# Expert attention of a two-layer vision tower: projection biases moved into the evacuation of the values, gate logits by column strips

## The chip, the cores and the metric

The kernel runs on one core of one Trainium2 chip, in one launch. The metric is the device time of one execution in microseconds. TensorE is called PE here, VectorE DVE, ScalarE ACT, GpSimd POOL and SyncE SP, as in the profile; PEld is TensorE's weight load, which overlaps its matmuls.

## The reference

A tokenizer turns 128 images into 64 tokens of 256 features each. Layer 0 is an attention with ReLU scores and then a feed-forward part that is itself an attention with experts; layer 1 is a linear attention and a mixture of experts. Everything is float32. The change lies in the feed-forward part of layer 0, which the program calls `expert_attention`. The reference writes it so (B = 128 images, T = 64 tokens, D = 256 features, E = 4 experts, C = 4 chunks of DC = 64 features, H = 2 heads of 32):

```python
xn = layernorm(x) * norm_w
gate = softmax(xn @ router_w.T + router_b, axis=-1)            # per token, over 4 experts
xc = xn.reshape(B, T, C, DC)
qkv = einsum('btcd,ekd->btcek', xc, qkv_w)                      # q, k, v per chunk, expert, head
attn = softmax(einsum('bcehtd,bcehsd->bcehts', q, k) * scale, axis=-1)
y = einsum('bcehts,bcehsd->bcehtd', attn, v)
y = einsum('btced,eod->btceo', y, proj_w) + proj_b              # proj_b: one bias of 64 per expert
out = einsum('btceo,bte->btco', y, gate).reshape(B, T, D)
return residual + out @ out_w.T
```

## The kernel before

The stages run one after another: tokenizer, ReLU attention, expert attention, linear attention, routing, experts. The residual stream `h2` stays in SBUF through the first three.

In `expert_attention` the unit of work is a **pair** of images: 2 x 64 tokens fill the 128 partitions. There are 64 pairs, and four pairs make a **block**, for which layer norm and gate are computed ahead. The projection `proj_w` is folded into the value weights before the loop (`wvp`, lines 766 to 783), so that a pair's values `v` are already projected. A softmax weight is multiplied by the gate of its expert (`weights`, lines 956 to 961), so that one sum over four experts and two heads (`mixed`) gives the gated output `z`; `output` multiplies it by `out_w` and adds it to `h2`. Softmax weights of a row sum to one, and so the bias `proj_b` reaches the output as gate times bias times `out_w`. The kernel before adds it there: before the loop it makes `bn` (bias times `out_w`, 4 x 256, placed at four row offsets), per block it transposes the gates into `gT` (lines 875 to 880), and per pair one more matmul (line 998) adds `gT` times `bn` to the output's PSUM tile `po`.

The order of the loop is written out by hand under a manual schedule, and each engine works through its own list in that order. One turn of the loop for pair p (`cur`), with the next pair (`new`) and the one before (`old`):

1. PE transposes `old`'s weights of head 0 (`pt`, line 970), ACT copies them out (973).
2. PE computes the scores `sc` (934); DVE takes maximum and difference of each head (946, 947).
3. PE computes queries and keys of `new` (`pqk`, 902), transposes `old`'s weights of head 1, computes the other half of `pqk`; ACT copies them out (906) and takes the exponents of the two heads (950).
4. DVE sums the exponents of each head and takes the reciprocal (953, 954); POOL scales (960, 961). Steps of other blocks that carry the place names "DVE", "DVE2" stand on DVE between or behind the two heads' sums: `statistics` (812, 813), `logits_less_max` (861 to 863), `sums` of the gate (869, 870).
5. PE mixes (`pz`, 983; ACT copies `z`, 991), computes `new`'s values into four PSUM tiles `pv` (914), and then `old`'s output `po` (997, 998). The values of chunk half `fc` = 0 (the first two `pv`) are copied to SBUF by ACT, those of `fc` = 1 by DVE (both on line 923). DVE adds `po` to `h2` (999).
6. PE does steps of other blocks at the place "PE" (transposes `ptx` 843, logits `pg` 854, gate transpose `pgt` 877).

All PSUM tiles but the scores come from one pool of four buffers of one bank each (tag "pq"), taken in turn, so that a matmul into a tile waits until the tile that is four places ahead of it has been read out. `po` takes the buffer of the first `pv`. A `pv` tile is 128 x 512 float32: its partitions are (expert pair, token), its free axis is (image, expert of the pair, head, 64 features).

The gate's logits of a block (line 854) are eight matmuls that hold `xT` (128 x 128) as weights and move four router columns each.

At which turn a block's steps stand is set by the `at` calls (lines 1014 to 1031) with n = 4b, the block's first pair; keys below zero are run before the loop ("first").

Of the kernel before, what the change touches and what calls it, by code (L numbers as in the profile page):

```python
# [11 lines left out]
F32 = mybir.dt.float32  # L12
# [7 lines left out]
P = 128  # L20
B = 128
T = 64
D = 256
# [30 lines left out]
def bcast(ap, axis, n):  # L54

    v = ap.unsqueeze(axis)
    shape = list(v.shape)
    shape[axis] = n
    return v.to_broadcast(shape)
# [670 lines left out]
def expert_attention(c, hd, normw, wr, br, wqkv, wvT, wproj, bproj, wout):  # L730
# [3 lines left out]
    tc, nc, h2 = c.tc, c.nc, c.h2  # L734
    SCALE = float(1.0 / np.sqrt(np.float32(32)))
    NP = B // 2
    NB = 4
    with (
# [7 lines left out]
    ):  # L746
        nw = wp.tile([P, 2], F32, name="nw")
        nc.sync.dma_start(nw, normw)
        wrs = wp.tile([P, 2, 4], F32, name="wrs")
        nc.sync.dma_start(wrs, wr.rearrange("(c p) e -> p c e", p=P))  # L750
        brs = wp.tile([P, 4], F32, name="brs")
        nc.sync.dma_start(brs, br.partition_broadcast(P))
        w = wp.tile([P, 2 * D], F32, name="w")
        bp2 = wp.tile([P, 4], F32, name="bp2")
        for k in range(2):
            nc.sync.dma_start(w[k * 64 : k * 64 + 64, :], wqkv)
            nc.sync.dma_start(bp2[k * 64 : k * 64 + 64, :], bproj)
        wv = wp.tile([32, 8, 64], F32, name="wv")
        nc.scalar.dma_start(wv, wvT)
        wpj = wp.tile([32, 8, 64], F32, name="wpj")  # L760
# [1 line left out]
        wo = wp.tile([P, 2, D], F32, name="wo")  # L762
# [7 lines left out]
        pv = psq.tile([P, 2, D], F32, tag="pq", name="pwv")  # L770
        for k in range(2):
            for e in range(4):
                for h in range(2):
                    r = (e % 2 * 2 + h) * 64
# [4 lines left out]
                        start=True,  # L779
                        stop=True,  # L780
                    )
        wvp = wp.tile([P, 2, D], F32, name="wvp")
        nc.vector.tensor_copy(wvp, pv)


        pb = psq.tile([4, D], F32, tag="pq", name="pb")
        for fc in range(2):
            nc.tensor.matmul(pb, bp2, wo[:, fc, :], start=(fc == 0), stop=(fc == 1))
        b4 = wp.tile([4, D], F32, name="b4")
        nc.vector.tensor_copy(b4, pb)  # L790
        bn = wp.tile([P, NB, D], F32, name="bn")
        nc.gpsimd.memset(bn, 0.0)
        for n in range(NB):
            nc.sync.dma_start(bn[4 * n : 4 * n + 4, n, :], b4)
        gTs = [wp.tile([P, P], F32, name=f"gT{k}") for k in range(3)]
        for gT in gTs:
            nc.gpsimd.memset(gT, 0.0)

        class Block:

            def __init__(self, p0):
                self.p0, self.gT = p0, gTs[p0 // NB % 3]

            def statistics(self, n0):
                if n0 == 0:
# [39 lines left out]
                nc.scalar.activation(self.xT[:, fc], self.pt, AF.Copy, scale=nw[:, fc : fc + 1])  # L848

            def logits(self):  # L850
                self.pg = pg = psq.tile([P, NB, 4], F32, tag="pq", name="pg")
                for n in range(NB):
                    for fc in range(2):
                        nc.tensor.matmul(
                            pg[:, n, :], self.xT[:, fc, n], wrs[:, fc, :], start=(fc == 0), stop=(fc == 1)
                        )

            def logits_less_max(self):
                self.gate = bp.tile([P, NB, 4], F32, tag="gate", name="gate")
# [11 lines left out]

            def gates(self):
                nc.gpsimd.tensor_mul(self.gate, self.gate, bcast(self.gm, 2, 4))

            def gates_transpose(self):
                self.pgt = psq.tile([4 * NB, P], F32, tag="pq", name="pgt")
                nc.tensor.transpose(self.pgt, self.gate.rearrange("p n e -> p (n e)"), c.ident)

            def gates_transposed(self):
                nc.scalar.copy(self.gT[0 : 4 * NB, :], self.pgt)  # L880

        class Pair:

# [24 lines left out]
            def values(self, fc):  # L908
                pv = [psq.tile([P, 2, D], F32, tag="pq", name="pv") for _ in range(2)]
                for j in range(2):  # L910
                    for eh in range(2):
                        for par in range(2):
                            r = slice(par * 64, par * 64 + 64)
                            nc.tensor.matmul(
                                pv[par][eh * 64 : eh * 64 + 64, j, :],
                                self.xT[r, fc, j * 64 : j * 64 + 64],
                                wvp[r, eh, :],
                                start=True,
                                stop=True,
                            )  # L920
                for par in range(2):
                    copy = nc.scalar.copy if fc == 0 else nc.vector.tensor_copy
                    copy(self.v[:, 2 * fc + par], pv[par])

            def scores(self):

# [66 lines left out]
            def output(self):  # L993
                p = self.p
                po = psq.tile([P, D], F32, tag="pq", name="po")
                for fc in range(2):
                    nc.tensor.matmul(po, self.z[:, fc], wo[:, fc, :], start=(fc == 0), stop=False)
                nc.tensor.matmul(po, self.blk.gT, bn[:, self.n, :], start=False, stop=True)
                nc.vector.tensor_add(h2[:, p], h2[:, p], po)
                if p % 4 == 3:  # L1000
                    nc.sync.dma_start(
                        hd[2 * p - 6 : 2 * p + 2].rearrange("(n b) t f -> (b t) n f", b=2),
                        h2[:, p - 3 : p + 1],
                    )
# [5 lines left out]
        def at(n, place, f, *a):  # L1010
            key = (n, place) if n >= 0 else "first"
            work.setdefault(key, []).append(lambda: f(*a))

        for b, x in enumerate(blocks):
            n = NB * b
            at(n - 11, "DVE", x.statistics, 0)
            at(n - 10, "DVE", x.statistics, 2)
            at(n - 9, "POOL", x.factors)
            for k in range(NB):
                at(n - 8 + k, "POOL", x.normal, k)  # L1020
            at(n - 4, "PE", x.transpose, 0)
            at(n - 3, "ACT", x.transposed, 0)
            at(n - 3, "PE", x.transpose, 1)
            at(n - 2, "ACT", x.transposed, 1)
            at(n - 2, "PE", x.logits)
            at(n - 1, "DVE", x.logits_less_max)
            at(n - 1, "ACT2", x.exponents)
            at(n - 1, "DVE2", x.sums)
            at(n - 1, "POOL", x.gates)
            at(n, "PE", x.gates_transpose)  # L1030
            at(n + 1, "ACT", x.gates_transposed)

        def do(key):
            for step in work.pop(key, ()):
                step()

        do("first")
        with tc.manual_schedule():
            old, cur = None, Pair(0, blocks[0])
            for fc in range(2):  # L1040
                cur.queries_keys(fc)
                cur.values(fc)
            for p in range(NP):
                new = Pair(p + 1, blocks[(p + 1) // NB]) if p + 1 < NP else None
                do((p, "ACT"))
                if old:
                    old.transposed(0)
                cur.scores()
                cur.less_max(0)
                cur.less_max(1)  # L1050
                if new:
                    new.queries_keys(0)
                if old:
                    old.transposed(1)
                cur.exponents(0)
                if new:
                    new.queries_keys(1)
                cur.exponents(1)
                cur.sums(0)
                cur.weights(0)  # L1060
                do((p, "DVE"))
                do((p, "ACT2"))
                cur.sums(1)
                cur.weights(1)
                do((p, "DVE2"))
                do((p, "POOL"))
                if old:
                    old.mixed()
                if new:
                    new.values(0)  # L1070
                    new.values(1)
                if old:
                    old.output()
                do((p, "PE"))
                old, cur = cur, new
            for x in range(2):
                old.transposed(x)
            old.mixed()
            do((NP, "ACT"))
            old.output()  # L1080
        assert not work

# [871 lines left out]
def layout(**i):  # L1954

    o = {}


    x = i["x"].reshape(B // 2, 2, 16, 8, 8, 2, 8)
    x = x.transpose(2, 5, 3, 6, 4, 1, 0).reshape(16, 2, 64, 8, B)  # L1960
    ev, od = x[:, :, :, 0::2], x[:, :, :, 1::2]
    x = [np.concatenate(y, axis=2) for y in ((ev[:, 0], od[:, 0]), (od[:, 1], ev[:, 1]))]
# [9 lines left out]
    q, k, v = (i[f"L0_attn_W{n}"].T for n in "qkv")  # L1972
# [11 lines left out]

    o["wvf"] = w[:, 2].reshape(8, 32, 64).transpose(1, 0, 2)
    o["wproj"] = i["L0_ffn_proj_w"].reshape(4, 64, 2, 32).transpose(3, 0, 2, 1).reshape(32, 8, 64)
    o["bproj"] = i["L0_ffn_proj_b"].T
    o["wout"] = i["L0_ffn_out_w"].T

    q, k, v = (i[f"L1_attn_W{n}"].T.reshape(D, 8, 32).transpose(0, 2, 1).reshape(D, D) for n in "qkv")  # L1990
    o["wqk1"], o["wv1"] = np.concatenate([q, k], axis=1), v
    q, k = (i[f"L1_attn_b{n}"].reshape(8, 32).T.reshape(D) for n in "qk")
# [27 lines left out]
```

## Time and profile before

| | us |
|---|---|
| runs: 2759.99, 2768.24, 2768.82; median | 2768.24 |
| profiled execution, whole | 2759.7 |
| its span, first to last instruction | 2757.9 |
| expert attention, from about 1104 to 1936 of the span | 832 |
| of it the loop, from the first scores to the last (1132.26 to 1917.31) | 785.05 |

The page counts busy time of each engine over the span: PE 2602.5, DVE 2038.5, POOL 1633.7, ACT 1628.9. In the stretch from 1237 to 1837, inside the loop, the granted TensorE clock was 1.00; the mean over the whole span was 0.971. A line of the timeline gives start, busy time, engine, source line, operation, written and read tiles, shapes and count; in brackets the idle time of the engine before it and what seems to have ended it. Runs of the same instruction are merged. A float32 matmul appears as two records.

### The profile page before, as it was taken

Reading aid. Unit: us, or ns where it says so; the run is one execution under the profiler, and the core shown is the slowest. Engines: PE = TensorE matmul, PEld = TensorE weight load, DVE = VectorE, ACT = ScalarE, POOL = GpSimd, SP = SyncE. Lnnn points to the kernel's source line nnn. Section 1 sums busy time; section 2 is a strip of 40 time slices with the busy share of each in tenths; the row PEclk is TensorE's granted clock in tenths of the full one; section 3 lists DMA queues with packets and bytes.
Section 4 is the critical chain, followed back from the end, with each engine's and each line's share of the span. In section 5 each row is a group of like instructions: output and inputs, shape, how many; then the busy total and the mean of one; then the engine's idle time right before and its main releaser. Section 6 shows DMA issues by size and latency. Waiting matters only on the chain. (4 is left out here: it accounts for less than half of the span.)

```text
span 2757.9 us, 76947 instructions
## 1 busy us (share of the span) xinstructions
PE 2602.5 (94%) x33263; PEld 1744.7 (63%) x33263; DVE 2038.5 (74%) x3024; ACT 1628.9 (59%) x3415; POOL 1633.7 (59%) x1390
## 2 busy tenths in 40 slices
PE   8989999999999998899999999999799986999997
PEld 4553444444444443688888888887466565888886
DVE  7769999999998998577778777777367775444443
ACT  3238888888888887466666565665245532233332
POOL 3329888888888887756565656543133312454444
PEclk9999999999999999899999999999899995999998
DMA  3000000000000000000000000000435443555554
GB/s 115 25 13 1 2 1 2 1 2 2 1 2 1 2 2 2 12 11 18 11 18 11 11 18 11 11 19 10 115 64 120 92 116 116 179 198 190 188 196 134
DMA packets 138063, 140.80 MB, mean 51 GB/s; under 512 B 107923, under 2 KB 121509, under 8 KB 130032
## 3 DMA queue, kind: packets, MB, share of 16 engines
q1 hardware_dynamic: 126816, 117.91, 14.3%
q0 software_dynamic: 7648, 14.77, 1.7%
q8 instruction: 263, 4.31, 0.7%
q10 hardware_dynamic: 3248, 3.09, 0.4%
q14 instruction: 88, 0.72, 0.1%
HBM read 103.93 MB, written 32.54 MB: 49 GB/s over the span
## 5 line engine op out<-in xcount | busy, mean ns | idle before, releaser
L495 POOL TENSOR_TENSOR m<-q,k 128x1024 f32<-128x1024 f32 x384 | 719.4, 1905 | 31.2 <-PE sc L297 16.1
L487 DVE TENSOR_TENSOR m<-pc,k 128x2048 f32<-128x2048 f32 (+1 forms) x320 | 646.5, 2057 | 0.5 <-ACT q L431 0.5
L297 PE MATMUL sc<-m,wide 128*32 128x512 f32 x4096 | 529.5, 598 | 12.0 <-DVE m L487 7.2
L496 ACT ACTIVATE m<-m 128x1024 f32<-128x1024 f32 x384 | 402.2, 1049 | 6.0 <-POOL m L495 5.5
L297 PEld LDWEIGHTS sc<-m,wide 128*32 128x32 f32 x4096 | 126.5, 109 | 259.7 <-issue 145.6
L505 ACT ACTIVATE m<-k,q 128x64 f32<-128x64 f32 x1024 | 270.8, 339 | 0.8 <-DVE k L378 0.8
L946 DVE TENSOR_REDUCE mx<-sc 128x16 f32<-128x1024 f32 x128 | 155.9, 1218 | 155.6 <-PE sc L934 125.3
L961 POOL TENSOR_TENSOR e<-e,mx 128x1024 f32<-128x1024 f32 x128 | 243.7, 1904 | 10.1 <-POOL mx L960 0.2
L906 ACT COPY qk<-pqk 128x512 f32<-128x512 f32 x256 | 138.7, 603 | 131.3 <-PE pqk L902 131.3
L960 POOL TENSOR_TENSOR mx<-mx,gate 128x16 f32<-128x16 f32 x128 | 27.8, 217 | 314.2 <-ACT z L991 155.3
L1854 PE MATMUL ph<-xt,w1s 128*128 128x256 f32 x896 | 201.0, 382 | 3.7 <-DVE xt L1845 3.1
L1870 PE MATMUL po<-w2s,hT 128*128 128x256 f32 x896 | 198.0, 379 | 0.0
L973 ACT COPY pT<-pt 128x512 f32<-128x512 f32 x256 | 138.7, 598 | 99.6 <-PE pt L970 98.7
L1854 PEld LDWEIGHTS ph<-xt,w1s 128*128 128x128 f32 x896 | 171.5, 192 | 28.9 <-DVE xt L1845 3.9
L1870 PEld LDWEIGHTS po<-w2s,hT 128*128 128x128 f32 x896 | 168.1, 190 | 21.7
L902 PE MATMUL pqk<-xT,w 64*128 64x128 f32 x2048 | 169.3, 289 | 1.3 <-issue 1.3
L947 DVE TENSOR_TENSOR e<-sc,mx 128x1024 f32<-128x1024 f32 x128 | 156.7, 1224 | 4.4
L1888 POOL DMA_INDIRECT out<-y,rout x56 | 56.8, 1014 | 168.4 <-ACT hT L1858 131.0
L1858 ACT ACTIVATE hT<-ph,w1s 128x256 f32<-128x256 f32 x224 | 93.5, 471 | 103.7 <-PE ph L1854 103.7
L902 PEld LDWEIGHTS pqk<-xT,w 64*128 64x128 f32 x2048 | 142.5, 189 | 18.9 <-issue 10.1
L953 DVE TENSOR_REDUCE mx<-e 128x16 f32<-128x1024 f32 x128 | 153.1, 1196 | 1.3 <-ACT e L950 1.1
L970 PE MATMUL pt<-ident,e 128*128 128x128 f32 x1024 | 143.3, 281 | 4.5 <-issue 0.9
(302 smaller groups left out, 4986.9 us busy)
## 6 DMA issues: line engine op xcount, KB each, us to landing
w1s<-in_we SPq DMA_DIRECT2D x30, 1028.0 KB, 5.2
w2s<-in_we SPq DMA_DIRECT2D x30, 1024.0 KB, 4.9
hd<-h SPq DMA_DIRECT2D x16, 512.0 KB, 3.2
x<-hd SPq DMA_DIRECT2D x16, 512.0 KB, 4.2
h<-hd SPq DMA_DIRECT2D x4, 2048.0 KB, 12.8
hx<-h SPq DMA_DIRECT2D x4, 2048.0 KB, 12.1
out<-h SPq DMA_DIRECT2D x4, 2048.0 KB, 21.3
xt<-in_x SPq DMA_DIRECT2D x15, 512.0 KB, 3.5
```

Of the source, the lines that this page charges most:

```text
L297: nc.tensor.matmul(dst[j : j + 32], wide[:, hf, s : s + 32], part, start=start, stop=stop)
L487: nc.vector.tensor_tensor(m, bcast(self.pq[:, hf, i : i + n], 3, T), k, ALU.max)
L495: nc.gpsimd.tensor_tensor(m, bcast(self.q[:, hf, s : s + 2], 3, T), k, ALU.subtract)
L496: nc.scalar.activation(m, m, AF.Relu)
L505: nc.scalar.activation(self.parts[i, hf][:, q], self.blk.k[:, hf, i], AF.Relu, bias=self.q[:, hf, i - NB // 2, q : q + 1], scale=-1.0,)
L902: nc.tensor.matmul(pq[par][:, k, eh, :], w[r, f : f + P], self.xT[r, fc], start=True, stop=True)
L946: nc.vector.tensor_reduce(mx, sc, AX.X, ALU.max)
L947: nc.vector.tensor_sub(e, sc, bcast(mx, 2, T))
L953: nc.vector.tensor_reduce(self.sm[x], self.e[x], AX.X, ALU.add)
L961: nc.gpsimd.tensor_mul(e, e, bcast(sm, 2, T))
L1854: nc.tensor.matmul(ph[:, j], self.w1[:, w0 : w0 + P], self.xt[:, fc], start=(fc == 0), stop=(fc == 1))
L1870: nc.tensor.matmul(po, self.hT[:, f, r * P : r * P + P], self.w2[:, f, :], start=(f == 0), stop=(f == 7))
```

## The change

1. The bias is added where the values leave PSUM. A tile `vb` (128 x 2 x 64) holds on each half of the partitions the biases of one pair of experts. Every one of a pair's four `pv` tiles is now evacuated in two halves: head 0 by a DVE addition of `vb`, head 1 by an ACT copy. Since a row's softmax weights over one head sum to one, adding the bias to one head's values alone adds it once.
2. With that `bn`, its set-up matmuls, copies and DMAs, the tiles `gT` with their memsets, the gate transposes (877, 880) and the third matmul of each pair's output (998) are gone.
3. The logits are computed with the router as weights (padded to 32 columns) and `xT` moving, in four column strips of one PSUM tile `pl`, eight matmuls; ACT copies the tile (`lg`), and one matmul with every 32nd group of four identity columns as the moving operand brings the logits back to tokens on partitions (`pg`). This last one stands at a new place "PE2", behind the second half of `pqk`.
4. All steps of a block are moved one pair earlier (`statistics` from n - 11 to n - 12, and so on), since the logits take one step more.

```diff
-        wrs = wp.tile([P, 2, 4], F32, name="wrs")
-        nc.sync.dma_start(wrs, wr.rearrange("(c p) e -> p c e", p=P))
+        wrs = wp.tile([P, 2, 32], F32, name="wrs")
+        nc.gpsimd.memset(wrs, 0.0)
+        nc.sync.dma_start(wrs[:, :, 0:4], wr.rearrange("(c p) e -> p c e", p=P))
...
+        vb = wp.tile([P, 2, T], F32, name="vb")
         for k in range(2):
             nc.sync.dma_start(w[k * 64 : k * 64 + 64, :], wqkv)
-            nc.sync.dma_start(bp2[k * 64 : k * 64 + 64, :], bproj)
+            nc.sync.dma_start(vb[k * 64 : k * 64 + 64], bproj[k].partition_broadcast(64))
...
-        pb = psq.tile([4, D], F32, tag="pq", name="pb")
-        for fc in range(2):
-            nc.tensor.matmul(pb, bp2, wo[:, fc, :], start=(fc == 0), stop=(fc == 1))
-        b4 = wp.tile([4, D], F32, name="b4")
-        nc.vector.tensor_copy(b4, pb)
-        bn = wp.tile([P, NB, D], F32, name="bn")
-        nc.gpsimd.memset(bn, 0.0)
-        for n in range(NB):
-            nc.sync.dma_start(bn[4 * n : 4 * n + 4, n, :], b4)
-        gTs = [wp.tile([P, P], F32, name=f"gT{k}") for k in range(3)]
-        for gT in gTs:
-            nc.gpsimd.memset(gT, 0.0)
...
             def logits(self):
-                self.pg = pg = psq.tile([P, NB, 4], F32, tag="pq", name="pg")
-                for n in range(NB):
-                    for fc in range(2):
+                self.pl = psq.tile([P, P], F32, tag="pq", name="pl")
+                for fc in range(2):
+                    for n in range(NB):
                         nc.tensor.matmul(
-                            pg[:, n, :], self.xT[:, fc, n], wrs[:, fc, :], start=(fc == 0), stop=(fc == 1)
+                            self.pl[n * 32 : n * 32 + 32],
+                            wrs[:, fc, :],
+                            self.xT[:, fc, n],
+                            start=(fc == 0),
+                            stop=(fc == 1),
                         )
+            def logits_copied(self):
+                self.lg = np_.tile([P, P], F32, tag="lg", name="lg")
+                nc.scalar.copy(self.lg, self.pl)
+
+            def logits_transpose(self):
+                self.pg = psq.tile([P, NB, 4], F32, tag="pq", name="pg")
+                some = c.ident.rearrange("p (n r) -> p n r", r=32)[:, :, 0:4]
+                nc.tensor.matmul(self.pg, self.lg, some, start=True, stop=True)
...
                 for par in range(2):
-                    copy = nc.scalar.copy if fc == 0 else nc.vector.tensor_copy
-                    copy(self.v[:, 2 * fc + par], pv[par])
+                    o, i = (x.rearrange("p j (e h o) -> p j e h o", e=2, h=2) for x in (self.v[:, 2 * fc + par], pv[par]))
+                    nc.vector.tensor_add(o[:, :, :, 0], i[:, :, :, 0], bcast(vb, 1, 2))
+                    nc.scalar.copy(o[:, :, :, 1], i[:, :, :, 1])
...
                 for fc in range(2):
-                    nc.tensor.matmul(po, self.z[:, fc], wo[:, fc, :], start=(fc == 0), stop=False)
-                nc.tensor.matmul(po, self.blk.gT, bn[:, self.n, :], start=False, stop=True)
+                    nc.tensor.matmul(po, self.z[:, fc], wo[:, fc, :], start=(fc == 0), stop=(fc == 1))
...
-            at(n - 11, "DVE", x.statistics, 0)
-            at(n - 10, "DVE", x.statistics, 2)
-            at(n - 9, "POOL", x.factors)
+            at(n - 12, "DVE", x.statistics, 0)
+            at(n - 11, "DVE", x.statistics, 2)
+            at(n - 10, "POOL", x.factors)
             for k in range(NB):
-                at(n - 8 + k, "POOL", x.normal, k)
-            at(n - 4, "PE", x.transpose, 0)
-            at(n - 3, "ACT", x.transposed, 0)
-            at(n - 3, "PE", x.transpose, 1)
-            at(n - 2, "ACT", x.transposed, 1)
-            at(n - 2, "PE", x.logits)
-            at(n - 1, "DVE", x.logits_less_max)
-            at(n - 1, "ACT2", x.exponents)
-            at(n - 1, "DVE2", x.sums)
-            at(n - 1, "POOL", x.gates)
-            at(n, "PE", x.gates_transpose)
-            at(n + 1, "ACT", x.gates_transposed)
+                at(n - 9 + k, "POOL", x.normal, k)
+            at(n - 5, "PE", x.transpose, 0)
+            at(n - 4, "ACT", x.transposed, 0)
+            at(n - 4, "PE", x.transpose, 1)
+            at(n - 3, "ACT", x.transposed, 1)
+            at(n - 3, "PE", x.logits)
+            at(n - 2, "ACT", x.logits_copied)
+            at(n - 2, "PE2", x.logits_transpose)
+            at(n - 2, "DVE", x.logits_less_max)
+            at(n - 2, "ACT2", x.exponents)
+            at(n - 2, "DVE2", x.sums)
+            at(n - 2, "POOL", x.gates)
...
                 if new:
                     new.queries_keys(1)
+                do((p, "PE2"))
                 cur.exponents(1)
```

The host's layout gives `bproj` as 2 x 128 instead of the transposed 64 x 4.

More of the change, by code (lines that the diff above doesn't have):

```diff
@@ L753, in expert_attention @@
         w = wp.tile([P, 2 * D], F32, name="w")
-        bp2 = wp.tile([P, 4], F32, name="bp2")
+        vb = wp.tile([P, 2, T], F32, name="vb")
         for k in range(2):
             nc.sync.dma_start(w[k * 64 : k * 64 + 64, :], wqkv)
-            nc.sync.dma_start(bp2[k * 64 : k * 64 + 64, :], bproj)
+            nc.sync.dma_start(vb[k * 64 : k * 64 + 64], bproj[k].partition_broadcast(64))
         wv = wp.tile([32, 8, 64], F32, name="wv")
@@ L783, in expert_attention @@
         nc.vector.tensor_copy(wvp, pv)
-        pb = psq.tile([4, D], F32, tag="pq", name="pb")
-        for fc in range(2):
-            nc.tensor.matmul(pb, bp2, wo[:, fc, :], start=(fc == 0), stop=(fc == 1))
-        b4 = wp.tile([4, D], F32, name="b4")
-        nc.vector.tensor_copy(b4, pb)
-        bn = wp.tile([P, NB, D], F32, name="bn")
-        nc.gpsimd.memset(bn, 0.0)
-        for n in range(NB):
-            nc.sync.dma_start(bn[4 * n : 4 * n + 4, n, :], b4)
-        gTs = [wp.tile([P, P], F32, name=f"gT{k}") for k in range(3)]
-        for gT in gTs:
-            nc.gpsimd.memset(gT, 0.0)
         class Block:
             def __init__(self, p0):
-                self.p0, self.gT = p0, gTs[p0 // NB % 3]
+                self.p0 = p0
             def statistics(self, n0):
@@ L873, in gates @@
                 nc.gpsimd.tensor_mul(self.gate, self.gate, bcast(self.gm, 2, 4))
[L875 to L880, printed above, removed]
         class Pair:
@@ L1078, in expert_attention @@
             old.mixed()
-            do((NP, "ACT"))
             old.output()
@@ L1986, in layout @@
     o["wproj"] = i["L0_ffn_proj_w"].reshape(4, 64, 2, 32).transpose(3, 0, 2, 1).reshape(32, 8, 64)
-    o["bproj"] = i["L0_ffn_proj_b"].T
+    o["bproj"] = i["L0_ffn_proj_b"].reshape(2, 2 * T)
     o["wout"] = i["L0_ffn_out_w"].T
```

## The prediction

> **What bounds the kernel now.** I read the page's busy times, then busy time by stage, then the loop's waits, then the timeline of one pair.
>
> ```profile
> PE 2602.5 (94%) x33263; PEld 1744.7 (63%) x33263; DVE 2038.5 (74%) x3024; ACT 1628.9 (59%) x3415; POOL 1633.7 (59%) x1390
> 1132.00:1936.00 804.00, 789.73 (x18112) 664.91 (x18104) 617.10 (x883) 492.13 (x888) 460.20 (x513) 0.99 0.04 13
> ```
>
> The second line is the expert attention's loop (columns: length, busy PE, PEld, DVE, ACT, POOL, granted clock, DMA share, GB/s). PE is busy 98%, DVE 77%. Of the waits between 1147 and 1919 (total us, times, longest):
>
> ```profile
> DVE mx L946 <- PE sc L934: 125.2, 51, 4.0
> PEld po L997 <- ACT v L923: 23.9, 62, 0.4
> ```
>
> DVE waits for the scores in nearly every pair; PE waits for nobody for longer than 0.4 us. That 0.4 is not a real wait either: 23.9 / 62 = 0.39 each time, whenever the copy ended, so it belongs to the step from the pv matmuls to po. PE is the bound, by a margin that one pair shows (1707.46 to 1720.59; its block also does statistics and logits here):
>
> ```profile
> 1707.46 1.46 PEld L934 LDWEIGHTS sc<-qk 32*64 32x64 f32 x128 [0.17 <-issue]
> 1709.09 1.22 DVE L946 TENSOR_REDUCE mx<-sc 128x16 f32<-128x1024 f32 x1 [2.19 <-PE sc L934]
> ...
> 1715.02 0.40 ACT L991 COPY z<-pz 128x256 f32<-128x256 f32 x1
> ...
> 1715.60 1.07 ACT L923 COPY v<-pv 128x512 f32<-128x512 f32 x2 [0.18 <-PE pv L914]
> ...
> 1716.33 1.19 DVE L953 TENSOR_REDUCE mx<-e 128x16 f32<-128x1024 f32 x1
> 1716.49 0.73 PEld L997 LDWEIGHTS po<-wo,z 128*128 128x128 f32 x4 [0.39 <-ACT v L923]
> ...
> 1717.24 0.41 PEld L998 LDWEIGHTS po<-bn,gT 128*128 128x128 f32 x2
> ...
> 1717.55 0.25 DVE L954 RECIPROCAL mx<-mx 128x16 f32<-128x16 f32 x1
> 1717.67 1.97 PEld L854 LDWEIGHTS pg<-wrs,xT 128*128 128x128 f32 x16
> 1717.71 1.22 DVE L923 COPY v<-pv 128x512 f32<-128x512 f32 x2
> ...
> 1718.85 0.41 DVE L999 TENSOR_TENSOR h<-h,po 128x256 f32<-128x256 f32 x1
> 1719.48 0.94 PEld L970 LDWEIGHTS pt<-ident,e 128*128 128x128 f32 x8
> ...
> 1720.59 1.46 PEld L934 LDWEIGHTS sc<-qk 32*64 32x64 f32 x128 [0.17 <-issue]
> ```
>
> Count from the scores' start (1707.46). DVE needs them: +1.63. It works without a gap through both heads and is free for values at +10.25 (1717.71). ACT empties the first two pv at +8.14, and po, which reuses the first pv's buffer, starts at +9.03. So before, PE passes DVE's sums: the values that DVE copies late are needed only by the transposes behind po.
>
> **What the change removes.** The bias matmul: 1717.24 to 1717.67, 0.43 us of PE per pair. The logits, 1717.67 to 1719.48, 1.81 us per block; the gate transpose, 0.11 (1693.53 to the next matmul at 1693.64). It adds per block eight strip matmuls (16 records). Nearest rows: pz, two column strips, 64 records in 2.08 us, 0.033 each, 0.52 in all; the old logits 1.81. I take 0.65, near pz by shape. The one matmul back (2 records) and ACT's copy of pl (about 0.3, while ACT idles) come to 0.25 of PE or nothing. On PE alone this would save about 0.43 x 4 + 1.0 = 2.7 us per block.
>
> **What it moves: the release of pv.** I read the built program's instruction order with each wait traced to what releases it. On DVE all four additions stand behind the second head's sum and reciprocal. Every ACT copy waits for the addition on the same pv tile, though they touch other heads. po waits for the first ACT copy, ptx or pl for the second, the two halves of pt for the third and fourth. Behind po in PE's order stand pt and the next scores, which DVE waits for. The loop is now closed: scores, DVE's two heads, addition, copy, po, pt, scores.
>
> Its legs: an addition like L999 (128x256, PSUM and SBUF) 0.42; the copy like L991 0.39; the handover between engines from these rows (gate ends at 1729.00, ACT starts 1729.04; z ends 1729.51, PEld starts 1729.56):
>
> ```profile
> 1728.83 0.17 DVE L863 TENSOR_TENSOR gate<-pg,gm 128x16 f32<-128x16 f32 x1
> 1729.04 0.21 ACT L866 ACTIVATE gate<-gate 128x16 f32<-128x16 f32 x1 [0.75 <-DVE gate L863]
> 1729.16 0.35 ACT L991 COPY z<-pz 128x256 f32<-128x256 f32 x1
> 1729.56 0.63 PEld L914 LDWEIGHTS pv<-wvp,xT 64*64 64x64 f32 x14 [0.32 <-ACT z L991]
> ```
>
> 0.04 and 0.06. Together 0.42 + 0.04 + 0.39 + 0.06, say 0.90 from DVE free (X) to po. Then po 0.75, what stands behind it, and pt 1.14 to the next scores (1.11 above, 1.14 in plain pairs). X is 10.32 with statistics (DVE's copy at 1705.36 in the pair from 1695.04), 9.20 without (1915.12 from 1905.92), 10.05 with the gate's maximum and sums (L870 of that pair ends at +10.07). A ptx adds 0.52 (in pairs where nothing waits; 0.55 at 1705.84). The four kinds of pair in the new order:
> - statistics and ptx: 10.32 + 0.90 + 0.75 + 0.52 + 1.14 = 13.63
> - statistics and pl: 10.32 + 0.90 + 0.75 + 0.65 + 1.14 = 13.76
> - gate: 10.05 + 0.90 + 0.75 + 1.14 = 12.84
> - ptx alone: 9.20 + 0.90 + 0.75 + 0.52 + 1.14 = 12.51
>
> Sum 52.74 against 11.94 + 12.18 + 13.13 + 12.36 = 49.61 of a regular block before: +3.13. The later pt do not wait: additions follow each other by some 0.33, so the third copy ends at X + 1.5 and pt asks at X + 1.65. Pairs 0 to 49 (twelve blocks and two pairs) give 660.3 against 619.4 regular, 625.2 in the trace (PE gaps marked "issue" and a slow start make the 5.8). The last 13 periods have no statistics: 161.8 against 159.8. So +37 if these 5.8 are absorbed by PE's new slack, +43 if they recur: I take +40.
>
> An addition that takes part of its neighbour's time, or costs the 0.68 of a 512 copy, moves 63 periods by -0.1 or +0.26: -6 to +16.
>
> **Start of the loop.** Moved one pair earlier, the second block's first transposes land before the loop, and in PE's list ahead of pair 0's pqk. They need the block's last two normalized tiles from POOL:
>
> ```profile
> 1130.51 2.44 POOL L835 TENSOR_SCALAR xn<-h,mv,ra 128x256 f32<-128x256 f32 x2
> 1132.26 1.46 PEld L934 LDWEIGHTS sc<-qk 32*64 32x64 f32 x128 [0.39 <-issue]
> ```
>
> They end at 1132.95; the memsets that go (0.96 + 0.50) bring 0.3 only, as statistics end then. From pqk's start to the scores it took about 6.8 (0.9 for six records at 1122.12, then 1126.35 to 1132.26). So the scores start at 1132.65 + 0.3 + 6.8 + 0.25 for the longer evacuation = 1140: +8, between 0 (if POOL's backlog of the first pairs shrinks as much) and +10. The set-up of bn lay beside POOL's work, and vb's two DMAs take the queue places of bp2's: nothing. If vb came late, the first additions (about 1136, 28 us after issue) would show it.
>
> **PE's clock.** PE will stand idle for 1 to 2.1 us per pair (pv ends at +9.10, po at X + 0.90). In the trace 1137.0 to 1140.7, with PE busy 2.03 of 3.70 us, was followed by 6.8 us at clock 0.50, in which the scores' load took 2.07 instead of 1.46, pt 1.57 instead of 0.94. So a dip costs about 1.2; 26 pairs with statistics make 0 to 31. I take 5, as 2263 to 2267 with PE busy 46% kept its clock.
>
> The Trainium skill ("TensorE: Matmul & The Clock Gate", Part 1) puts the drop at an idle window of about 3.4 us, longer than any of these gaps; by it this term would be 0 and the forecast 2808.
>
> The skill also speaks against the split itself: "PSUM — Partial Sum Buffer" (Terms, PSUM bank) says no two engines may access one bank within a partition in the same cycle. A pv tile is one bank, so by it the halves cannot run side by side, as the built order has it. No row here shows two engines in one bank.
>
> **Sum.** +40 + 8 + 5 - 0.4 (last pair's bias matmul) = +53 on the profiled execution's 2759.7: 2813. That execution is the fastest seen, 8.5 below the median 2768.24; runs of the change may scatter upward likewise, which the range takes in.
>
> **The rivals.**
> - *PE stays the bound (faster).* For it: DVE idles 125 us on the scores, and PE loses 2.7 us of work per block. It decides if the additions are done by po's old time, X below 8.1; then blocks take 11.44 + 11.57 + 11.9 + 11.44 = 46.35, -41 over pairs 0 to 49, -11 behind, +8: 2716. Against it: X is 9.20 at the least, since the additions stand behind both sums. 4%.
> - *The additions cost, the copies do not* (they run beside them). Then 0.43 per period less, 63 x 0.43 = 27: 2786. Against it: the traced waits. 4%.
> - *Clock dips in most statistics pairs*: 25 more: 2838. For it the dip at 1140. 17%.
> - My case: 73%. Some mixture that ends within 8 us of before: 2%.
>
> A measurement tells about 0.3%, 8 us. Faster 0.04, same 0.02, slower 0.94. The range from 2785 (copies hidden, or cheap additions and no start cost) to 2842 (dips).
>
> **What would show it.** In the trace of the changed kernel: PEld po waits 1.0 to 2.1 us per pair for ACT's copy, 80 to 100 us in all; periods of a block 13.6, 13.8, 12.8, 12.5; DVE's wait on the scores stays about 2 us, as both stretch; first scores near 1140; PE busy in the loop falls to about 90%. I am wrong if po starts before DVE's second reciprocal ends, or if DVE's wait on scores vanishes; the clock term if the loop's granted clock is below 0.97.

## The result, and the profile after

| | before | after |
|---|---|---|
| median of the runs, us | 2764.49 (4 runs, 2759.99 to 2768.82) | 2833.74 (4 runs, 2830.38 to 2834.81) |
| profiled execution; its span | 2759.7; 2757.9 | 2834.8; 2833.0 |
| the loop, first scores to last | 785.05 | 841.47 |

The ratio is 1.025 (95% interval 1.0232 to 1.0269): slower by 2.5%. The forecast was 2813 with a range of 2785 to 2842.

The 75.1 us between the two spans come apart at three places in the trace. The last transpose of the ReLU attention (`pto`, line 459, code that the change does not touch) ends at 1106.88 before and at 1114.24 after: 7.4. From there to the first scores it takes 25.4 before and 36.2 after: 10.8. The loop is 56.4 longer, and what follows it 0.5.

First the page's busy times of the changed kernel, and the loop as one stretch (length, busy PE, PEld, DVE, ACT, POOL, granted clock, DMA share, GB/s):

```profile
PE 2585.3 (91%) x33147; PEld 1718.1 (61%) x33147; DVE 2048.2 (72%) x3151; ACT 1650.2 (58%) x3543; POOL 1632.7 (58%) x1387
1150.00:1980.00 830.00, 741.36 (x17435) 616.36 (x17428) 608.20 (x986) 498.58 (x988) 442.09 (x490) 0.97 0.04 12
```

PE is busy for 17 us less, and 89% of the loop (741.36 of 830) instead of 98%. No engine is full now: this is a loop of waits. The waits of the same stretch (total us, times, longest) name it:

```profile
DVE mx L943 <- PE sc L931: 163.9, 62, 4.5
ACT v L920 <- DVE v L919: 128.6, 63, 3.1
PEld po L994 <- ACT v L920: 107.6, 61, 2.5
```

Read them upwards: po waits for ACT's copy, the copy for DVE's addition, and DVE, once round, for the scores. One pair with statistics and the logits, from its scores on (the next ones start at 1665.60):

```profile
1651.68 1.64 PEld L931 LDWEIGHTS sc<-qk 32*64 32x64 f32 x128 [0.33 <-issue]
...
1658.86 2.10 PE L910 MATMUL pv<-wvp,xT 64*64 64x256 f32 x32
...
1661.95 0.25 DVE L951 RECIPROCAL mx<-mx 128x16 f32<-128x16 f32 x1
1662.12 1.35 DVE L919 TENSOR_TENSOR v<-pv,vb 128x256 f32<-128x256 f32 x4
...
1662.52 1.37 ACT L920 COPY v<-pv 128x256 f32<-128x256 f32 x4 [2.69 <-DVE v L919]
...
1662.94 1.13 PE L994 MATMUL po<-wo,z 128*128 128x256 f32 x4 [1.98 <-ACT v L920]
...
1664.00 0.64 PE L844 MATMUL pl<-xT,wrs 128*32 128x128 f32 x16
```

PE ends pv at 1660.96 and stands until 1662.94. In that time DVE comes to its second reciprocal, adds (1662.12), ACT copies 0.40 later, po starts 0.42 after that. Before, po started at +9.03 from the scores; here at 1662.94 - 1651.68 = +11.26 (in an undisturbed pair of this kind +11.07).

### The profile page after: what moved, and what is told of

It reads as the page before. It is cut to its first block, busy times and chain, and to the rows that moved or that the text cites. A ratio compares the mean times of both kernels' runs of the same rounds, so it can differ in the third digit from the quotient of the medians.

```text
span 2833.0 us, 76947 instructions
## 1 busy us (share of the span) xinstructions
PE 2585.3 (91%) x33147; PEld 1718.1 (61%) x33147; DVE 2048.2 (72%) x3151; ACT 1650.2 (58%) x3543; POOL 1632.7 (58%) x1387
## 5 line engine op out<-in xcount | busy, mean ns | idle before, releaser
L920 ACT COPY v<-pv 128x256 f32<-128x256 f32 x256 | 87.3, 373 | 132.3 <-DVE v L919 132.3
L994 PE MATMUL po<-wo,z 128*128 128x256 f32 x256 | 77.2, 427 | 84.1 <-ACT v L920 80.7
```

## The experiments

For each kernel the periods of a regular block are given in the order of its pairs p mod 4 = 0 to 3, read from the starts of the scores in its trace; in the changed kernel these are 13.52, 13.74, 12.77, 12.39 (sum 52.42), in the kernel before 11.94, 12.18, 13.13, 12.36 (49.61).

**1. Whole evacuation again.** The changed kernel with

```diff
-                    o, i = (x.rearrange(...) for x in (self.v[:, 2 * fc + par], pv[par]))
-                    nc.vector.tensor_add(o[:, :, :, 0], i[:, :, :, 0], bcast(vb, 1, 2))
-                    nc.scalar.copy(o[:, :, :, 1], i[:, :, :, 1])
+                    copy = nc.scalar.copy if fc == 0 else nc.vector.tensor_copy
+                    copy(self.v[:, 2 * fc + par], pv[par])
```

> The changed kernel with one thing undone: the four pv tiles are evacuated whole again, fc 0 by ACT, fc 1 by DVE. The bias is then added nowhere (it is left out of the result; a whole copy costs what it did before). Theory (the loop closes through DVE's reciprocal, its addition, ACT's copy, po): po now waits only for ACT's early copy, so PE no longer waits for it; pt waits for DVE's first whole copy, 0.72 us behind the reciprocal. Periods of a block: two statistics pairs 10.32 + 0.72 + 1.14 = 12.18 each, gate 11.91, ptx alone 11.44 by PE's own work, sum 47.7 against 52.4 regular in the changed kernel; no clock dips in the loop. Over 63 periods that is about -90: 2745 us, faster than the kernel before by 0.7 per cent. Rival (the loss is in the strip logits, the moved schedule or DVE's whole work, not in who evacuates what): within 10 us of 2834. Rival (half of it): 2790.

Measured: 2739.94 us, ratio to before 0.9921 (0.9901 to 0.9941). Periods 12.18, 12.12, 11.93, 11.40, sum 47.63. Its timeline in a pair with the gate:

```profile
1513.86 1.13 PE L993 MATMUL po<-wo,z 128*128 128x256 f32 x4
1513.97 1.29 DVE L919 COPY v<-pv 128x512 f32<-128x512 f32 x2
```

po starts before DVE's copies do, since ACT alone frees its buffer. So the whole loss, and more, goes with these three lines; what is left of the change (strips, schedule, no bias matmul, and here no bias at all) is a gain of 0.8%.

**2. The split alone.** The kernel before with the three split lines, and a `vb` that is set to zeros by a memset.

> The kernel before with the split evacuation alone: head 0 by a DVE addition of a tile of zeros, head 1 by an ACT copy, for all four pv tiles. The bias matmul, the old logits and the old schedule stay. Theory: all of the change's loss and more, since PE's removed work is back behind po: with X as in the kernel before, 0.82 from X to po and 1.14 for pt, periods 9.20+0.82+1.18+0.52+0.11+1.14 = 12.97, 10.32+0.82+1.18+0.52+1.14 = 13.98, 10.32+0.82+1.18+1.81+1.14 = 15.27, 10.05+0.82+1.18+1.14 = 13.19, sum 55.4 against 49.6. Over 63 periods +78: 2843 us without clock dips, about 2862 with as many as in the changed kernel. Start of the loop within 2 us of the kernel before. Rival (the split is hidden and something else costs): 2764 within 10.

Measured: 2860.71 us, ratio 1.0341 (1.0317 to 1.0365). Periods 12.93, 13.94, 15.18, 13.20, sum 55.25 (55.4 expected). Its waits in the loop have the same line, against 107.6 above:

```profile
PEld po L1000 <- ACT v L926: 109.3, 62, 2.5
```

The split does it alone. What the change took off PE (bias matmul, old logits) stood behind po and shortened the closed loop by 55.25 - 52.42 = 2.8 us per block.

**3. Statistics behind the output.** The changed kernel with

```diff
-            at(n - 12, "DVE", x.statistics, 0)
-            at(n - 11, "DVE", x.statistics, 2)
+            at(n - 12, "DVE3", x.statistics, 0)
+            at(n - 11, "DVE3", x.statistics, 2)
...
                 if old:
                     old.output()
+                do((p, "DVE3"))
                 do((p, "PE"))
```

> The changed kernel with the layer norm's statistics moved on DVE from between the two heads' sums to behind the addition of po, so that they no longer stand ahead of the value additions. Nothing else. Theory: X falls from 10.3 to 9.2 in the 26 pairs with statistics, -1.1 each, -29 us; PE's idle gap in these pairs falls from about 2.0 to 0.95 us, and with it go the clock dips, some -20: 2834 - 47 = 2787. If the dips stay: 2806. Rival (X does not set po, or DVE is bound by its whole work): 2834 within 6.

Measured: 2781.79 us, ratio 1.0072 (1.0053 to 1.0092). Periods 12.39, 12.68, 12.78, 12.39: -1.13 and -1.06 in the pairs with statistics, nothing in the others. The granted clock from 1210 to 1940 is 1.00 (0.97 in the changed kernel from 1210 to 1990). DVE does the same work; only its place moved (a pair with statistics):

```profile
1515.91 1.13 PE L994 MATMUL po<-wo,z 128*128 128x256 f32 x4 [0.93 <-ACT v L920]
...
1517.42 0.42 DVE L801 BATCH_NORM_STATS2 st<-h 128x6 f32<-128x256 f32 x1
...
1519.92 1.22 DVE L943 TENSOR_REDUCE mx<-sc 128x16 f32<-128x1024 f32 x1 [1.27 <-PE sc L931]
```

PE's gap ahead of po is 0.93 us, where pairs of this kind (statistics and ptx) had 2.05 in the changed kernel. The statistics (801) now stand where DVE would wait for the scores: 1.27 us of that wait are left.

**4. A filler for PE.** The changed kernel with one matmul more, ahead of `old.output()`:

```diff
+                if p % 4 < 2:
+                    idle = pss.tile([P, 2, 8, T], F32, tag="sc", name="idle")
+                    nc.tensor.matmul(idle[:, 0].rearrange("p c s -> p (c s)"), cur.xT[:, 0], w, start=True, stop=True)
```

> The changed kernel with one more matmul (128 x 512, its result is never read) in PE's order between values and po, in the pairs with statistics: it fills about half of PE's idle gap there and waits for nothing recent. Theory (the clock falls because PE stands idle for 2 us, and that costs some 20 us of the loop): clock of the loop back to 1.00, statistics pairs back to 13.5 from about 15, total 2834 - 20 = 2814, although PE does more work. Rival (the clock falls for another reason, or its dips cost nothing in a loop that PE does not bound): 2834 within 5. If the matmul does not fit the gap: up to +26.

Measured: 2815.16 us, ratio 1.0181 (1.016 to 1.0202): faster than the changed kernel with 64 PE records more. Regular periods are unchanged (13.52, 13.74, 12.77, 12.39), but pairs that took 14.9 to 15.2 in the changed kernel now take 13.52. The window from 1740 to 1840 in the filler's kernel,

```profile
1740.00:1840.00 100.00, 92.03 (x2160) 73.78 (x2152) 73.40 (x123) 59.05 (x119) 59.77 (x67) 1.00 0.04 13
```

and in the changed kernel (the granted clock is the third number from the end):

```profile
1740.00:1840.00 100.00, 88.95 (x2022) 73.50 (x2020) 71.78 (x119) 58.17 (x115) 51.84 (x54) 0.95 0.04 13
```

So the clock's drops (the granted clock falls to 0.50 for one or more stretches of 3.41 us) cost 17.3 us of loop (841.47 - 824.13; by the medians 18.6), although PE does not bound the loop: po, pt and the scores' load are legs of the closed chain, and at half clock they are longer.

**5. The copy first.** The changed kernel with the addition and the copy of a tile exchanged:

```diff
-                    nc.vector.tensor_add(o[:, :, :, 0], i[:, :, :, 0], bcast(vb, 1, 2))
                     nc.scalar.copy(o[:, :, :, 1], i[:, :, :, 1])
+                    nc.vector.tensor_add(o[:, :, :, 0], i[:, :, :, 0], bcast(vb, 1, 2))
```

> The changed kernel with ACT's copy of head 1 written ahead of DVE's addition of head 0, on each pv tile. ACT then copies when the pv matmuls end, and po waits for DVE's addition alone. Theory (addition and copy of one tile stand one behind the other, whichever is first): from X to po 0.48 us instead of 0.82, -0.34 in each of 63 periods, -21 us: 2813; some more if the shorter idle gap (1.7 instead of 2.05 us) ends some clock dips: 2795 to 2813. Rival (the copies already run beside the additions, so their order is nothing): 2834 within 5.

Measured: 2787.54 us, ratio 1.0087 (1.0071 to 1.0104): a larger gain than expected. Periods 13.11, 13.33, 12.37, 11.99: -0.40 everywhere. A pair with statistics:

```profile
1513.72 0.65 ACT L919 COPY v<-pv 128x256 f32<-128x256 f32 x2 [0.19 <-PE pv L910]
...
1515.91 1.35 DVE L920 TENSOR_TENSOR v<-pv,vb 128x256 f32<-128x256 f32 x4
...
1516.33 1.13 PE L994 MATMUL po<-wo,z 128*128 128x256 f32 x4 [1.65 <-DVE v L920]
```

ACT copies as soon as PE has filled a tile, long before DVE comes; po follows the first addition by 0.42 instead of 0.82. And with PE's gap at 1.65 us instead of 2.05 the drops of the clock are gone as well (first period excepted): 63 x 0.40 = 25 and some 17 make the 41.8 by which the loop is shorter.

**6. The schedule one pair later.** The changed kernel with every `at(n - k, ...)` as `at(n - k + 1, ...)`.

> The changed kernel with all steps of a block one pair later, at the pairs of the kernel before (statistics at n - 11 and so on). Theory (the moved schedule costs at the start alone: transposes of the second block ahead of pair 0's queries wait for POOL's normals): first scores about 12 us earlier, periods of the loop unchanged in kind, total 2834 - 12 = 2822. Rival (the loop's start is set elsewhere, by the split evacuation): 2834 within 3. Rival (the gate, one pair nearer to its use, now comes late): above 2834.

Measured: 2820.75 us (2807.93 to 2827.28), ratio 1.0207 (1.0182 to 1.0232). From the last `pto` to the first scores it takes 22.4 us instead of 36.2; the undisturbed periods of the loop are the same four numbers, one pair on. So step 4 of the change, alone, costs the start 13.8. The trace shows this; the total, whose runs lie 19 us apart, shows it only just.

**7. The strips alone.** The kernel before with parts 3 and 4 of the change; its gate transposes stay, one pair earlier like the rest.

```diff
+            at(n - 1, "PE", x.gates_transpose)
+            at(n, "ACT", x.gates_transposed)
```

> The kernel before with the strip logits (copy and transpose back included) and the schedule one pair earlier alone: bias matmul, gate transposes and whole evacuation stay. Theory (PE bounds this kernel, so what the strips save on PE counts): logits 0.65 + 0.25 instead of 1.81, -0.9 in each of some 15 blocks, -14 in the loop; the start of the loop +11 by the earlier schedule; together 2761 - 3 = 2758, between 2752 and 2764. Rival (the longer gate chain sets the gate pair): loop not shorter, 2772. Rival (schedule costs nothing at the start): 2747.

Measured: 2771.07 us, ratio 1.0031 (1.0019 to 1.0044): the number is that of the first rival, but not its mechanism. The loop gained what was expected (769.38, -15.7), while the start took 47.3 us from the last `pto` instead of 25.4. PE's timeline there:

```profile
1148.95 0.38 PE L892 MATMUL pgt<-ident,gate 128*16 128x128 f32 x1 [18.16 <-POOL gate L888]
...
1150.12 2.08 PE L917 MATMUL pqk<-xT,w 64*128 64x128 f32 x16
```

My edit had put the first block's gate transpose ahead of pair 0's queries, and its gates stand on POOL behind the normalized tiles of the second block and the first of the third: PE waits 18 us.

**8. The bias without the split.** The changed kernel with

```diff
+                    if fc == 0:
+                        nc.scalar.copy(self.v[:, par], pv[par])
+                    else:
+                        nc.vector.tensor_add(self.v[:, 2 + par], pv[par], bcast(vz, 1, 2))
+            def biased(self):
+                for par in range(2):
+                    o = self.v[:, par].rearrange("p j (e h o) -> p j e h o", e=2, h=2)[:, :, :, 0]
+                    nc.gpsimd.tensor_add(o, o, bcast(vb, 1, 2))
```

in place of the three split lines (`vz` is `vb` with zeros for head 1; `biased` of the next pair stands behind its values), with the statistics of run 3 and the schedule of run 6.

> A version of the change without its loss: no bias matmul, strip logits, but whole evacuations as in the kernel before: fc 0 copied by ACT, its bias added later in SBUF by POOL (128 x 256, twice per pair); fc 1 by one DVE addition of the bias padded with zeros for head 1; statistics behind the addition of po; the block's steps at the pairs of the kernel before. Theory (then PE bounds the loop again and its removed work counts): per block 0.43 x 4 + 0.9 + 0.1 = 2.7 us less than before, over 63 periods -43, start as before: 2761 - 43 = 2718. Rival (POOL's 1.2 us more per pair delays its weights, and pt waits for them): above 2750. Rival (DVE's second reciprocal and whole additions set pt): about 2735.

Measured: 2724.99 us, ratio 0.9861 (0.984 to 0.9881): faster than both kernels. Periods 11.67, 11.40, 11.69, 11.93, sum 46.69; the loop 746.14 (-38.9; -43 expected, 3.3 of the difference in the first pair, part of it at half clock). From its timeline:

```profile
1520.88 1.13 PE L1004 MATMUL po<-wo,z 128*128 128x256 f32 x4
...
1521.05 1.23 DVE L925 TENSOR_TENSOR v<-pv,vz 128x512 f32<-128x512 f32 x2
...
1527.12 1.41 POOL L930 TENSOR_TENSOR v<-v,vb 128x256 f32<-128x256 f32 x2
```

po waits for nobody again; DVE's addition over 512 takes what its copy took (1.23 for two; 1.22 before), and POOL's 1.41 us per pair lie between its other steps, a whole pair ahead of their use.

**9. The strips at the old pairs.** Run 7 with the steps of a block, the gate transposes included, at the pairs of the kernel before.

> The kernel before with the strip logits alone, as in the run on the strips, but with the steps of a block at the pairs of the kernel before. Theory (in the run on the strips the loop gained 15.7 us and the start lost 22, because the first block's gate transpose then stood ahead of pair 0's queries and waited for POOL): the loop's gain stays and the start is within 2 us of the kernel before: 2763 - 16 = 2747. Rival (the start is lost by the strips themselves): 2771 again. Rival (the longer gate chain is now late for its pair): loop gain halved or gone, 2755 to 2763.

Measured: 2750.94 us, ratio 0.9958 (0.9945 to 0.997). Start 23.7 us from the last `pto`, periods 11.94, 12.18, 12.12, 12.36, sum 48.60: the logits' pair is 1.01 shorter, the others as before; the loop, 773.06, is 12.0 shorter (15.7 in run 7, whose periods have the same sum). Part 3 of the change is a small gain, and run 7's loss was the place of one transpose.

**10. The split mended.** The changed kernel with the edits of runs 3, 5 and 6 together.

> The changed kernel with its split evacuation, and the three single mendings together: statistics behind the addition of po, ACT's copy ahead of DVE's addition on each tile, the block's steps one pair later. Theory (each took its own leg out of the same loop): X 9.2 in all pairs but the gate's, 0.41 from X to po, periods 11.99, 12.28, 12.37, 11.99, sum 48.6; over 63 periods 771 us, start 3 us earlier than the kernel before: 2763 - 17 = 2746. Rival (the loop meets another bound, PE's own work or POOL): 2755 or more. The version with POOL's bias stays faster (2725) as there the additions are no part of the loop at all.

Measured: 2749.12 us, ratio 0.995 (0.9934 to 0.9966). Periods 11.98, 11.99, 12.27, 12.36, sum 48.60. The wait of po in its loop, against 107.6 in the changed kernel:

```profile
PEld po L994 <- DVE v L920: 56.4, 61, 1.0
```

The three mendings add up. The loop is 24.9 us longer than run 8's; per block 1.9 us. That is the gap of PE ahead of po in the four pairs of a block: 0.52, 0.52, 0.52 and 0.37 us in its trace, and none in run 8's.

## Why the prediction was right, and where its sizes were off

The mechanism stands: the closed loop over scores, DVE, addition, copy, po, pt. Runs 1 and 2 show that the split is its cause, alone and whole; runs 3 and 5 each shorten one leg of it, and the time falls by that leg. None of the rivals in which PE stays the bound or the copies are free happened: the first addition, the copy and po stand one behind the other.

**Periods.** Predicted 13.63, 13.76, 12.84, 12.51, sum 52.74; measured where the clock held 13.52, 13.74, 12.77, 12.39, sum 52.42. The leg from X (DVE free) to po is 0.82 (1662.12 to 1662.94), not 0.90: the copy starts 0.40 behind the addition's start and po 0.42 behind the copy's. The rows that I took were a little too long: the first of the four additions took 0.36 here instead of 0.42, and a copy 0.37 instead of 0.39. The strips took 0.64 (0.65 predicted). Run 4, in which the clock held, has a loop of 824.13, 39.1 longer than before; the term was +40. That it came so close is luck in part: by the measured periods pairs 0 to 49 take 656.3 and not 660.3, and of the 5.8 us of irregular time, which I had counted half, 4.9 came back (661.2 in run 4's trace). Run 5 measures the leg once more: without the copy's 0.40 every period is 0.40 shorter. Whether two engines could read one pv tile at once, which "PSUM — Partial Sum Buffer" (Terms, PSUM bank) rules out, no run shows: the built order lets none try. Addition and copy also write one tile `v`; which of the two shared tiles makes the built order wait, no run separates.

The signs that I had named: po's wait came to 107.6 us by the weight loads (80 to 100), PE's share of the loop to 89% (about 90). DVE's wait on the scores grew from 125.2 us (51 times, 2.5 us each, where I had written about 2) to 163.9 (62 times, 2.6 us each); half-clocked po, pt and scores are in it.

**Start of the loop.** Predicted +8, measured +10.8. The place is the one predicted: pair 0's queries stand behind `ptx` of the second block, the last of which waits for POOL until 1140.16.

```profile
1140.57 2.08 PE L898 MATMUL pqk<-xT,w 64*128 64x128 f32 x16
...
1150.45 1.59 PE L931 MATMUL sc<-qk 32*64 32x64 f32 x128
```

1140.57 less the 7.4 of the earlier stages is 1133.2, and I had put the queries' start at 1132.65 + 0.3 = 1132.95. What was mis-sized is the way from there to the scores: 9.88 instead of 6.8 + 0.25. The granted clock was 0.50 in all of it, as in the 21 us ahead of it, in which PE mostly waited for POOL; before, it was 0.65 in the last 5.91 us. A window of the changed kernel and one of the kernel before:

```profile
1140.57:1150.45 9.88, 9.68 (x65) 6.42 (x64) 0.76 (x2) 2.85 (x6) 7.90 (x14) 0.50 0.01 2
```

```profile
1126.35:1132.26 5.91, 5.91 (x59) 3.94 (x59) 0.88 (x5) 3.29 (x7) 5.91 (x6) 0.65 0.01 3
```

Run 6 takes the whole term away.

**PE's clock.** Predicted +5 with a range of 0 to 31, measured 17 to 19 by run 4. This is the term that was furthest off. I took 5 because a stretch of another stage had kept its clock with PE, as I had it, busy 46%, and one with 55% had lost it; these were stretches of my own choosing, and the first was misread: from 2263 to 2267 PE is busy 1.41 of 4.00 us, which is 35%. My sign for this term, a loop clock below 0.97, was too coarse: the loop shows 0.97. The trace's clock changes lie on a grid of 3.41 us. Two neighbouring pairs, each with its gap, cut on that grid:

```profile
1645.33:1648.74 3.41, 1.36 (x15) 0.82 (x8) 3.03 (x8) 1.26 (x4) 3.04 (x3) 1.00 0.00 0
1648.74:1652.15 3.41, 3.41 (x46) 2.89 (x45) 0.42 (x1) 1.73 (x4) 3.15 (x3) 0.50 0.45 153
1658.98:1662.39 3.41, 1.98 (x32) 1.22 (x32) 3.27 (x9) 0.84 (x2) 2.23 (x3) 1.00 0.00 0
1662.39:1665.81 3.42, 2.87 (x51) 2.12 (x59) 1.50 (x5) 2.12 (x7) 3.24 (x4) 1.00 0.00 0
```

In the first window PE is busy 1.36 us, since its gap of 2.05 lies wholly in it, and the next window runs at 0.50. The second gap, 1.98, is cut by the grid into 1.43 and 0.55; both windows are busier, and the clock holds. So it was in the stretch at 2263 of the kernel before: its gap is even 2.98 us, but the grid cuts it at 2263.74, PE is busy 1.99 and 1.56 us in the two windows, and the clock holds. A window at half clock cost a pair 1.4 to 1.7 us, not the 1.2 that I took. So the rival of dips "in most statistics pairs" came half true: 12 windows behind the first pair, ten of them in pairs with statistics and ptx, and the one that I called likeliest was too mild. That 2833.74 lies in the range is owed to its upper end, which was put there for these dips.

"TensorE: Matmul & The Clock Gate" of the Trainium skill, Part 1, gives half rate after an idle window of some 3.4 us; read as a gap of that length, its clock term was 0 and its forecast 2808, and the measurement decides against that reading: gaps of 2.05 us were enough. The same part says that the window is free-running and 3413 ns long; the grid agrees (eight times two drops of the changed kernel stand 54.61 us apart, 16 times 3.413).

**What is no part of the change.** 7.4 of the 75.1 us were lost in stages that both kernels share. The same end of `pto` stood between 1107.06 and 1116.11 in the profiled executions of runs 1 to 10, with no relation to the edit that could be seen, and the runs of the kernel before spread alike (2759.99 to 2768.82). I had named this scatter without a number in the sum. Against the profiled 2759.7, then, 53 was forecast and 75 found: 7 of scatter, 12 to 14 of clock drops, 3 of the start at half clock, -1 of the periods.

## What to carry to other kernels

When work on PSUM tiles is handed to a second engine, look at what stands ahead of it in that engine's list and who waits behind: here 0.4 us of addition and 0.4 us of copy closed a loop that had been open, and cost 4.8 to 5.6 us per block (runs 1 and 2), although in the changed kernel every engine has time to spare. Put the engine that is free early on the tile that is needed early, and work that nobody waits for (the statistics, the bias) behind the step that somebody waits for. Where PE gets a gap of 2 us, expect the clock to fall in some of the turns (here in 12 of the 25 pairs with a gap of about that length), and price that from windows on the clock's own grid.

## What the runs showed of the hardware that I had not expected

- In the loops of all twelve profiled kernels (from the fourth pair on), cut on the 3.41 us grid of each trace, 24 of the 25 drops from full to half clock followed a window with PE busy between 1.33 and 1.53 us; in the other one the records show 2.02. The least busy window that was not followed by a drop had 1.46. So in these loops the bound lies near 1.45 of 3.41 us. It is no rule for other code: in the kernel before, the clock also fell behind windows with PE busy 1.84 us (1137.34 to 1140.75, in the first pair) and, in the linear attention, 2.50 and 2.53 us (2188.65 to 2192.06, 2198.89 to 2202.30); what counts there, no run shows. Runs 3 and 5 (longest regular gaps 0.93 and 1.65 us) kept their clock behind the first pair.
- Whether a gap costs anything depends on where it falls on the grid. A block with one drop takes about 54.1 us (15.19, 13.74, 12.77, 12.39), close to 16 windows (54.61), and in the changed kernel drops follow one another block by block, eight times 54.61 us apart. In run 6 they came in 7 of the pairs, and its runs spread over 19 us (that the one makes the other is not shown); run 2, with the same gaps and a block of 55.25 us, had only 6 stretches at half clock behind its first pair.
